# Raw output weights in four tiles instead of one, and their squares in four parts

## The chip, the cores and the metric

The kernel runs on one core of one Trainium2 chip. The metric is the device time of one execution in microseconds; three executions of the kernel before took 661.33, 661.75 and 663.46 us, so its time is the median, 661.75 us. The profile is of one execution more.

An engine's name in the profile stands for: PE, TensorE's matrix products, and PEld, its loading of weights; DVE, VectorE; ACT, ScalarE; POOL, GpSimd; SP, SyncE, which issues the DMAs.

## The reference

One decoder layer over 8 sequences of 128 tokens of width 512, in float32. Three blocks, each added to the residual `x`:

```python
x = x + attn(layernorm(x), w_q, w_k, w_v, w_o)        # 32 query heads, 8 key/value heads, of 128; causal
x = x + xattn(ctx, ctx, layernorm(x))                 # one head over the 128 context rows
x = x + ffn(layernorm(x), gate, up, down)             # 4-bit weights; silu(gate) * up, inner width 1376
```

What matters here is the first block's end. With `P[h]` the softmax of the masked and scaled scores of head `h`, the block adds

```python
attn = concat_h(P[h] @ V[h // 4])     # [8, 128, 4096]
x    = x + attn @ w_o                 # w_o: [4096, 512], 8 MB
```

so each group of 4 query heads that shares a key/value head multiplies its own 512 rows of `w_o`, 1 MB.

## The kernel before, in words

**Numbers.** Each product of two float32 matrices is made of three float16 products: both factors are split into a high and a low half (`split`, lines 116 and 119, and `convert`), and `mm3` (lines 162 to 164) adds high x high, high x low and low x high in PSUM. Before it is split a weight is multiplied by a scale that keeps it in float16's range. The scale of a block of weights comes from its sum of squares: `sumsq` squares the block on ScalarE and lets ScalarE sum along the row into one column of `ss` (line 260; what is written out, `junk`, is not used), and `scales_parts` casts the columns to bfloat16 (`sb`, line 283), adds them over rows and columns with one-column matmuls against a matrix of constants (`ps_n`, line 287 or 290), and makes the scale of it (lines 296 to 312, `sco` for the output weights). `convert` then multiplies the raw weights by the scale in place on GpSimd (line 356), casts them on ScalarE (`woh`) and subtracts on GpSimd (`wol`). Two of the 32 blocks are converted directly, on ScalarE and VectorE (lines 350 and 351), and read the raw weights without writing them.

**Units and steps.** The attention goes through 16 units, pairs of a group of heads (8) and a half of the batch (2 x 4 sequences); each unit has 4 steps, one a sequence: 64 steps. A unit is followed by the other half of its group; of the last two groups first both first halves run, and then both second halves. In step `i` the kernel makes the scores of step `i+1` (`att_s`), a piece of the projections for the unit after (`proj_piece`), the output product of step `i-1` (`att_o`, `ps_o`) and the product of probabilities and values of step `i` (`att_v`, `ps_at`, cast and split into `ah` and `al`). The scores are masked and scaled on VectorE (line 607), exponentiated on ScalarE (564), multiplied by the reciprocal sums on GpSimd (574 and 621), split (`pb`) and transposed by a DMA from SyncE (`pt`, line 635).

**Weights.** What a step has to prepare of coming weights is written in a table, filled by `at(step, ...)` in a loop over the groups (lines 1115 to 1142) and read at the end of each step. For the output weights of group `g`, whose first unit has number `u0`, with `c = 4 * (u0 - 1)` and `m = c - 4`: the load is issued at step `m`, the squares are made at `m + 1` and `m + 2`, the scale at `m + 3`, and the four blocks of 128 rows are converted at `c` to `c + 3` (`prep_wo`). A step below zero counts as 0. For groups 2 to 6, `m` is the step after the one in which the previous group's last block is converted. For group 7, `m` is the step in which group 6's first block is converted. Group 0 is loaded, squared and scaled in the opening (`begin`), which writes its instructions' order out by hand on every engine.

**Places.** A tile with `bufs=1` has one place in SBUF; whoever writes it next must wait until everything that reads it is done. `rawo` is one such tile of 128 x 4 x 512 float32. The load of group `g` so waits until the last of the four blocks of group `g - 1` has been converted, by `wol` on GpSimd as a rule.

**Order.** The program states no order beyond what data and places ask, but for the opening, and for a few edges: `issue_after` puts a square behind the exponentials, and a multiply of the raw weights behind the multiply of the probabilities, of the step that has just been written (`pace`). A planner that simulates the engines with its own estimates of durations then lays down a fixed order for each engine and for SyncE's issues; at run time every engine and SyncE take their instructions in that order and wait where something is not ready. From step 53 on GpSimd's order, and TensorE's until step 59, follow the text.

**DMAs.** Nearly all go out from SyncE: the weight loads, `pt`, duplicates of values (`vd`), and, in steps 8 to 41, the pieces of the quantized feed-forward weights and their zeros (`qr` and `zi`, lines 790 and 798).

Of the kernel before, what the change touches and what calls it, by code (L numbers as in the profile page):

```python
# [8 lines left out]
F32 = mybir.dt.float32  # L9
# [8 lines left out]
P = 128  # L18
HQ = 64
B = 8  # L20
H = 512
KT = 4
NG = 8
GH = 4
NH = 32
HB = 4
TH = 512
# [26 lines left out]
def tile_decoder(  # L54
# [19 lines left out]
    nc = tc.nc  # L74

    def pool(name, bufs=1, **kw):
        return tc.alloc_tile_pool(name=name, bufs=bufs, **kw)
# [12 lines left out]
    for k in range(2):  # L90
        m = const.tile([P, (k + 1) * HQ], F32, name=f"mask{k}")
# [95 lines left out]
    def bank(tag, shape, name):  # L187
        return psum.tile(shape, F32, name=name, tag=tag, bufs=BANKS[tag])
# [7 lines left out]
    rawp = pool("raw", 2)  # L196
# [13 lines left out]
    raw_t = {}  # L210
    sc_t = {}
# [22 lines left out]
        )  # L234

    def fetch_wo(g):
        raw_t["o", g] = raw = rawp.tile([P, GH, H], F32, name="rawo", tag="rawo", bufs=1)
        nc.sync.dma_start(
            raw, wo[g * TH : (g + 1) * TH, :].rearrange("(j p) c -> p j c", p=P)
        )  # L240

    def sumsq(kind, g, i, j, n=1):

        raw = raw_t[kind, g]
        if kind == "q":
            view = raw[:, :, j * P : (j + 1) * P]
        elif kind == "c":
            view = raw.unsqueeze(1)
        elif kind in "kv":
            view = raw  # L250
        else:
            view = raw[:, i * GH // n : (i + 1) * GH // n, :]
        key = "ss", kind, g
        if key not in raw_t:
            cols = GH if kind == "q" else n
            raw_t[key] = small.tile([P, cols], F32, name="ss" + kind, tag="ss" + kind)
        col = j if kind == "q" else i
        junk = work.tile([P, 2 * TH], BF16, name="junk", tag="junk", bufs=1)
        free = view.shape[1] * view.shape[2]
        ins = nc.scalar.activation(  # L260
            junk[:, :free].rearrange("p (a t) -> p a t", a=view.shape[1]),
            view,
            AF.Square,
            accum_out=raw_t[key][:, col : col + 1],
        )
        if pace:
            issue_after(ins, pace["exp"])
        return ins
# [79 lines left out]
    def convert(hi, lo, raw, sc, direct=False):  # L348
        if direct:
            a = nc.scalar.activation(hi, raw, AF.Copy, scale=sc)  # L350
            b = nc.vector.scalar_tensor_tensor(lo, raw, sc, hi, ALU.mult, ALU.subtract)
            return a, b
        wide = sc
        while len(wide.shape) < len(raw.shape):
            wide = wide.unsqueeze(2)
        a = nc.gpsimd.tensor_tensor(  # L356
            raw, raw, wide.to_broadcast(list(raw.shape)), ALU.mult
        )
        if pace:
            issue_after(a, pace["mul"])  # L360
        b, c = split(hi, lo, raw, nc.gpsimd)
        return a, b, c
# [21 lines left out]
    def prep_wo(g, j, direct=False):  # L384
        hi = wop.tile([P, H], F16, name="woh", tag="woh")
        lo = wop.tile([P, H], F16, name="wol", tag="wol")
        wo_t[g * GH + j] = hi, lo
        return convert(hi, lo, raw_t["o", g][:, j, :], sc_t["o", g], direct)

    def transpose4(src, tag):  # L390
        ps = bank(tag, [P, KT, P], "ps_x")
# [423 lines left out]
    for m in "gud":  # L815
        _, _, _, ngr, n = quant[m]
# [9 lines left out]
    def begin():  # L826

        warm = const.tile([P, TH], BF16, name="warm")
        nc.vector.memset(warm, 0.0)
        psw = bank("s", [P, TH], "ps_w")  # L830

        def fill(n):
            for _ in range(n):
                nc.tensor.matmul(psw, warm[:, :P], warm, start=True, stop=True)

        fill(11)
        load_x(0)
        load_x(1)
        fetch_wk(0)
        for b in range(2, HB):  # L840
            load_x(b)
        fetch_wq(0)
        fetch_wv(0)
        for b in range(HB, B):
            load_x(b)
        fetch_wo(0)
        fetch_wk(1)

        kgen = k_wide(0)
        h = {b: h_wide(b) for b in range(HB)}  # L850
        two = slice(0, TH // 2), slice(TH // 2, TH)
        q = [proj_q(0, 0, j, two if j == 0 else (slice(0, TH),)) for j in range(GH)]
        v = [proj_v(0, b) for b in range(HB)]
        ln_stats(0)
        ln_apply(0)
        ln_stats(1)
        ln_apply(1)
        sumsq("k", 0, 0, 0)
        next(h[0])
        fill(4)  # L860
        sk = scales_parts("k", 0)
        ln_stats(2)
        ln_apply(2)
        next(h[0])
        next(h[0])
        next(sk)
        next(h[1])
        fill(2)
        ln_stats(3)
        ln_apply(3)  # L870
        next(kgen)
        next(h[1])
        next(h[0])
        next(h[1])
        next(h[1])
        next(sk)
        next(h[2])
        next(kgen)
        sumsq("q", 0, 0, 0)
        next(h[2])  # L880
        next(h[2])
        sq0 = scales_parts("q", 0, (0, 1))
        next(sq0)
        sumsq("q", 0, 0, 1)
        next(h[3])
        next(kgen)
        next(sq0)
        next(h[3])
        next(h[2])
        sq1 = scales_parts("q", 0, (1, 2))  # L890
        next(sq1)
        next(h[3])
        prep_wq(0, 0, True)
        sumsq("q", 0, 0, 2)
        next(sq1)
        next(h[3])
        next(kgen)
        next(q[0])
        prep_wq(0, 1, True)
        sumsq("q", 0, 0, 3)  # L900
        sq = scales_parts("q", 0, (2, GH))
        ln_stats(4)
        ln_apply(4)
        next(q[0])
        next(sq)
        next(sq)
        next(kgen)
        prep_wq(0, 2, True)
        next(q[0])
        sumsq("v", 0, 0, 0)  # L910
        prep_wq(0, 3, True)
        h_dma(4)
        sv = scales_parts("v", 0)
        next(q[1])
        next(sv)
        ln_stats(5)
        ln_apply(5)
        next(q[1])
        next(sv)
        ln_stats(6)  # L920
        ln_apply(6)
        prep_wv(0, 0, True)
        h_dma(5)
        next(q[2])
        prep_wv(0, 1, True)
        next(q[2])
        ln_stats(7)
        ln_apply(7)
        h_dma(6)
        soft_scale(0)  # L930
        next(q[3])
        next(q[3])
        last_h = h_dma(7)
        fetch_wq(1)
        next(v[0])
        n = len(nc.cur_bb.bb.instructions)
        att_s(0, 0)
        loose.update(
            i.name for i in nc.cur_bb.bb.instructions[n:] if i.engine != mybir.EngineType.PE
        )  # L940
        next(v[1])
        next(v[0])
        prep_wk(0, True)
        next(v[2])
        next(v[1])
        next(v[3])
        next(v[2])
        next(v[3])
        run(proj_k(0, 1))
        run(proj_q(0, 1, 0))  # L950
        so = scales_parts("o", 0)
        for i in range(2):
            sumsq("o", 0, i, 0, 2)
        run(so)
        out_scale(0)
        prep_wo(0, 0, True)
        prep_wo(0, 1, True)
        return last_h

# [152 lines left out]
    def at(step, *fs):  # L1112
        todo.setdefault(max(step, 0), []).extend(fs)

    for g in range(1, NG):
        u0 = units.index((g, 0))
        c = HB * (u0 - 2)
        if g > 1:
            m = c - HB
            at(m, lambda g=g: fetch_wk(g))  # L1120
            at(m + 1, lambda g=g: (fetch_wq(g), sumsq("k", g, 0, 0)))
            at(m + 2, lambda g=g: (sumsq("q", g, 0, 0), sumsq("q", g, 0, 1)))
            at(m + 3, lambda g=g: (sumsq("q", g, 0, 2), sumsq("q", g, 0, 3)))
            at(m + 3, lambda g=g: (scales("q", g), scales("k", g), soft_scale(g)))
        for j in range(GH):
            at(c + j, lambda g=g, j=j: prep_wq(g, j))
        at(c + 1, lambda g=g: prep_wk(g))
        c = HB * (u0 - 1)
        m = c - HB
        at(m, lambda g=g: fetch_wo(g))  # L1130
        at(m + 1, lambda g=g: sumsq("o", g, 0, 0, 2))
        at(m + 2, lambda g=g: sumsq("o", g, 1, 0, 2))
        at(m + 3, lambda g=g: (scales("o", g), out_scale(g)))
        for j in range(GH):
            at(c + j, lambda g=g, j=j: prep_wo(g, j))
        if g % 2 == 0:
            c = HB * (u0 - 3)
            at(c - 2, lambda g=g: fetch_wv(g // 2))
            at(c - 1, lambda g=g: sumsq("v", g // 2, 0, 0))
            at(c, lambda g=g: scales("v", g // 2))  # L1140
            at(c + 2, lambda g=g: prep_wv(g // 2, 0))
            at(c + 3, lambda g=g: prep_wv(g // 2, 1))
# [332 lines left out]
```

## Time and profile before

| | us |
|---|---|
| median of three executions (from, to) | 661.75 (661.33, 663.46) |
| profiled execution, whole | 663.5 |
| its span, first to last instruction | 661.7 |
| TensorE busy | 631.9 |
| VectorE busy | 471.0 |
| ScalarE busy | 441.3 |
| GpSimd busy | 391.4 |
| 8 loads of `rawo`, 1 MB each, issue to landing where it is recorded | 5.6 |
| 16 squares of 128 x 1024 of `rawo`, median of one | 1.049 |
| 32 squares of 128 x 512 of `rawq`, median of one | 0.628 |

A line of a timeline or a group names the line of the kernel, the engine, the operation, what is written and read (`woh,ah` are the operands of `ps_o`), the shape, and how many; brackets at the end hold the idle time of the engine before it and who ended it. A matrix product's end is modelled and overlaps the next one's start, so holes in TensorE's work are best read from start to start. In the answer for one tile, the first list is time in which the engine of such an instruction sat idle before it, by what ended the wait, and the second is time in which others sat idle for it.

### The profile page before, as it was taken

The numbers are of one execution on the slowest core, as the hardware profiler recorded it, in microseconds if no ns is written. First come the engines' busy times: TensorE is split into PE (matmuls) and PEld (weight loads), VectorE is DVE, ScalarE is ACT, GpSimd is POOL, SyncE is SP. The second block draws the span as 40 slices with busy tenths as digits, with TensorE's granted clock in tenths as the row PEclk, the third lists the DMA queues.
The fourth block names the chain that finished last, engine by engine and source line by source line (L and its number), as shares of the span: only waits on it lengthen the run. The fifth ranks groups of instructions, "written<-read, shape, count | busy, mean of one in ns | idle before, by whom it ended". The sixth has DMA issues, their size and how long they took to land.

```text
span 661.7 us, 12423 instructions
## 1 busy us (share of the span) xinstructions
PE 631.9 (95%) x3992; PEld 340.9 (52%) x3992; DVE 471.0 (71%) x1476; ACT 441.3 (67%) x1240; POOL 391.4 (59%) x581
## 2 busy tenths in 40 slices
PE   8889999899999999999999999999998988999996
PEld 5545545455655555555555565455554444445443
DVE  6846786556767776675767565777676668978897
ACT  5676677565758574666678566865566478876674
POOL 6658497664747795556588597753577247621521
PEclk9999999999999999999999999999999999999999
DMA  8266244945453855445546514243534243102002
GB/s 309 49 162 163 87 46 131 235 99 158 120 158 83 187 133 153 108 148 140 156 115 146 148 37 124 47 103 69 88 61 70 41 87 53 32 17 63 2 1 63
DMA packets 117773, 69.34 MB, mean 105 GB/s; under 512 B 84190, under 2 KB 100593, under 8 KB 117708
## 3 DMA queue, kind: packets, MB, share of 16 engines
q1 hardware_dynamic: 117708, 68.55, 42.7%
q8 instruction: 31, 0.51, 0.3%
q14 instruction: 34, 0.28, 0.1%
HBM read 42.12 MB, written 2.20 MB: 67 GB/s over the span
## 4 chain that ended last, share of the span: by engine, by line
PE 49%; POOL 15%; DMA 10%; DVE 9%; issue 8%; ACT 7%; SPq 0%; DVEq 0%; POOLq 0%; ACTq 0%
PE ps_c L1176 6%; PE ps_c L1177 6%; PE ps_o L164 5%; PE ps_o L162 5%; PE ps_o L163 5%; PE ps_q L164 4%; PE ps_q L163 4%; PE ps_q L162 4%; DMA pt<-pb 3%; POOL pb L119 3%; DMA rawq<-in_L_attn_w_q_dram 3%; POOL s L621 3%; DMA rawo<-in_L_attn_w_o_dram 2%; POOL wql L119 2%; ACT junk L260 2%
## 5 line engine op out<-in xcount | busy, mean ns | idle before, releaser
L564 ACT ACTIVATE s<-s,negm 128x64 f32<-128x64 f32 (+1 forms) x256 | 93.0, 365 | 32.8 <-DVE negm L607 32.5
L162 PE MATMUL ps_o<-woh,ah 128*128 128x512 f16 x256 | 97.1, 379 | 2.3 <-ACT ah L116 2.2
L162 PE MATMUL ps_q<-hT,wqh 128*128 128x512 f16 (+1 forms) x260 | 97.7, 376 | 1.4 <-ACT wqh L350 1.4
L164 PE MATMUL ps_o<-woh,al 128*128 128x512 f16 x256 | 97.0, 379 | 1.2 <-DVE al L119 1.2
L164 PE MATMUL ps_q<-hT,wql 128*128 128x512 f16 (+1 forms) x260 | 97.7, 376 | 0.0
L163 PE MATMUL ps_q<-hT,wqh 128*128 128x512 f16 (+1 forms) x260 | 97.7, 376 | 0.0
L163 PE MATMUL ps_o<-wol,ah 128*128 128x512 f16 x256 | 97.0, 379 | 0.0
L119 POOL TENSOR_TENSOR pb<-s,pb 128x256 f16<-128x256 f32 (+1 forms) x128 | 71.7, 576 | 13.0 <-ACT pb L116 10.6
L661 DVE SCALAR_TENSOR_TENSOR xr<-ps_o,unsc,xr 128x512 f32<-128x512 f32 x64 | 47.8, 747 | 41.7 <-PE ps_o L164 41.1
L574 POOL TENSOR_SCALAR rec<-rec 128x4 f32<-128x4 f32 x64 | 14.8, 231 | 95.5 <-DVE rec L572 93.7
L607 DVE CUSTOM_DVE_ANT_0 s<-ps_sc,mask,soft 128x64 f32<-128x64 f32 (+1 forms) x256 | 66.8, 310 | 5.3 <-PE ps_sc L164 2.5
L621 POOL TENSOR_TENSOR s<-s,rec 128x128 f32<-128x128 f32 (+1 forms) x128 | 63.8, 519 | 4.5
L119 DVE TENSOR_TENSOR ql<-ps_q,qh 128x512 f16<-128x512 f32 x64 | 43.9, 686 | 31.2 <-ACT qh L116 31.0
L116 ACT CAST pb<-s 128x256 f16<-128x256 f32 (+1 forms) x128 | 43.0, 350 | 31.7 <-POOL s L621 29.1
L116 ACT CAST ah<-ps_at 128x512 f16<-128x512 f32 x64 | 37.1, 581 | 23.2 <-PE ps_at L164 9.5
L119 DVE TENSOR_TENSOR al<-ps_at,ah 128x512 f16<-128x512 f32 x64 | 43.7, 683 | 6.7 <-ACT ah L116 6.2
L564 ACT ACTIVATION_READ_ACCUMULATOR s<-s,negm 128x1 f32 x256 | 48.2, 188 | 0.0
L116 ACT CAST qh<-ps_q 128x512 f16<-128x512 f32 x64 | 36.7, 573 | 13.9 <-PE ps_q L164 13.9
L1189 DVE TENSOR_SCALAR ps_c<-ps_c,rTg 128x512 f32<-128x512 f32 (+1 forms) x56 | 40.6, 750 | 7.0 <-PE ps_c L1177 6.0
L1187 ACT ACTIVATE ps_c<-ps_c,rTu 128x512 f32<-128x512 f32 (+1 forms) x57 | 36.3, 659 | 13.7 <-PE ps_c L1177 11.8
L356 POOL TENSOR_TENSOR rawo<-rawo,sco 128x512 f32<-128x512 f32 x30 | 31.4, 1053 | 22.2 <-DVE sco L312 20.1
L164 PE MATMUL ps_sc<-k,ql 128*128 128x64 f16 (+1 forms) x256 | 42.8, 206 | 1.0 <-DVE ql L119 1.0
(239 smaller groups left out, 1725.9 us busy)
## 6 DMA issues: line engine op xcount, KB each, us to landing
rawq<-in_L_attn_w_q_dram SPq DMA_DIRECT2D x8, 1024.0 KB
rawo<-in_L_attn_w_o_dram SPq DMA_DIRECT2D x8, 1024.0 KB, 5.6
zi<-zd SPq DMA_DIRECT2D x26, 256.0 KB, 4.1
vd<-v SPq DMA_DIRECT2D x64, 64.0 KB, 2.9
qr<-_L_ffn_down_qweight_dram SPq DMA_DIRECT2D x10, 256.0 KB
xr<-in_x_dram SPq DMA_DIRECT2D x8, 256.0 KB, 8.6
rawk<-in_L_attn_w_k_dram SPq DMA_DIRECT2D x8, 256.0 KB, 4.4
rawv<-in_L_attn_w_v_dram SPq DMA_DIRECT2D x4, 512.0 KB
```

The costliest lines, as they stand in the source:

```text
L116: a = nc.scalar.copy(hi, src)
L119: b = (lo_eng or nc.vector).tensor_tensor(lo, src, hi, ALU.subtract)
L162: nc.tensor.matmul(ps, lh, rh, start=start and i == 0, stop=False)
L163: nc.tensor.matmul(ps, lh, rl, start=False, stop=False)
L164: nc.tensor.matmul(ps, ll, rh, start=False, stop=stop and i == n - 1)
L564: exp = nc.scalar.activation(v, v, AF.Exp, bias=negm[:, j : j + 1], scale=-1.0, accum_out=sums[:, j : j + 1],)
L607: nc.vector.tensor_tensor_reduce(view, flat(ps, cols[j]), masks[j // 2], soft_t[g][:, j % 2 : j % 2 + 1], BIG, ALU.add, ALU.min, negm,)
L621: mul = nc.gpsimd.tensor_tensor(v, v, rec[:, 2 * k : 2 * k + 2].unsqueeze(2).to_broadcast([P, 2, (k + 1) * HQ]), ALU.mult,)
L661: return nc.vector.scalar_tensor_tensor(xr[b], ps, unsc_t[g], xr[b], ALU.mult, ALU.add)
L1176: nc.tensor.matmul(ps, lh, rh, start=r == 0, stop=False, skip_group_check=r > 0)
L1177: nc.tensor.matmul(ps, lh, rl, start=False, stop=True, skip_group_check=r > 0)
L1189: nc.vector.tensor_scalar(ps, ps, sc, None, ALU.mult)
```

## The change

`rawo` becomes four tiles of 128 x 512 float32, with tags `rawo0` to `rawo3`, each with one place of its own; together they take the room of the one before. A new function, `fetch_wo_part`, loads one of them, 256 KB. In the table, part `j` of a group is loaded at step `m - 3 + j`; so the parts of groups 2 to 6 are asked for one by one in the step after that in which the previous group's block `j` is converted (`fetch_wo`, which loads all four, remains for group 0). For group 7 the steps are 41 to 44, and group 6's blocks are converted in steps 44 to 47, so there each part has to wait for its place. For group 1 the four steps are all step 0.

The sum of squares is made of four parts of 512 elements, at steps `m`, `m + 1`, `m + 1` and `m + 2`, with four columns in `ss` and so four one-column matmuls in `scales_parts` (whose code is not touched). The scale stays at `m + 3` and the conversions at `c` to `c + 3`. In the opening group 0 is loaded by four DMAs and squared in four parts.

```diff
     def fetch_wo(g):
-        raw_t["o", g] = raw = rawp.tile([P, GH, H], F32, name="rawo", tag="rawo", bufs=1)
-        nc.sync.dma_start(
-            raw, wo[g * TH : (g + 1) * TH, :].rearrange("(j p) c -> p j c", p=P)
-        )
+        for j in range(GH):
+            fetch_wo_part(g, j)
+
+    def fetch_wo_part(g, j):
+        raw = rawp.tile([P, H], F32, name="rawo", tag=f"rawo{j}", bufs=1)
+        raw_t.setdefault(("o", g), []).append(raw)
+        nc.sync.dma_start(raw, wo[g * TH + j * P : g * TH + (j + 1) * P, :])
...
-            view = raw[:, i * GH // n : (i + 1) * GH // n, :]
+            view = raw[i].unsqueeze(1)
...
-        return convert(hi, lo, raw_t["o", g][:, j, :], sc_t["o", g], direct)
+        return convert(hi, lo, raw_t["o", g][j], sc_t["o", g], direct)
...
-        for i in range(2):
-            sumsq("o", 0, i, 0, 2)
+        for j in range(GH):
+            sumsq("o", 0, j, 0, GH)
...
-        at(m, lambda g=g: fetch_wo(g))
-        at(m + 1, lambda g=g: sumsq("o", g, 0, 0, 2))
-        at(m + 2, lambda g=g: sumsq("o", g, 1, 0, 2))
+
+        for j in range(GH):
+            at(m - 3 + j, lambda g=g, j=j: fetch_wo_part(g, j))
+        for j in range(GH):
+            at(m + j - (j > 1), lambda g=g, j=j: sumsq("o", g, j, 0, GH))
         at(m + 3, lambda g=g: (scales("o", g), out_scale(g)))
         for j in range(GH):
             at(c + j, lambda g=g, j=j: prep_wo(g, j))
```

## The prediction

> **What bounds the kernel now.** I read first the page's busy times and its chain, then the waits of TensorE, then everything that touches the raw output weights (`rawo`), then the timelines of the engines where that showed a wait, and last the SyncE queue.
>
> From the page:
>
> ```profile
> PE 631.9 (95%) x3992; PEld 340.9 (52%) x3992; DVE 471.0 (71%) x1476; ACT 441.3 (67%) x1240; POOL 391.4 (59%) x581
> ...
> PE 49%; POOL 15%; DMA 10%; DVE 9%; issue 8%; ACT 7%; SPq 0%; DVEq 0%; POOLq 0%; ACTq 0%
> ```
>
> TensorE does work that the change leaves alone; the time can only fall by the holes between its matmuls. In a dense stretch 512-column matmuls start 0.22 us apart, so I count a hole from start to start. Between 40 and 500 us the holes over 0.4 us that could have to do with `rawo` are: 0.77 us at 66.50, 1.10 at 89.86, 1.84 at 124.25, 0.48 at 232.83, 1.71 at 415.36, 0.49 at 430.49. The other large ones lie after 440 us, in the last attention steps, cross attention and the feed-forward network.
>
> The answer for the tile `rawo`:
>
> ```profile
> its engine sat idle before it (us, times) until:
>   DVE sco L312: 20.1, 4
>   POOL rawo L356: 7.3, 13
>   DMA rawo<-in_L_attn_w_o_dram: 5.8, 2
> ...
>   ACT junk L260: 5.8, 2
> ```
>
> ScalarE twice stood still for the 1 MB load: 4.0 us before the square at 64.78 (load issued at 56.68, for group 1) and 1.8 us before the one at 411.64 (issued at 405.79, for group 7). The ScalarE timeline around the second:
>
> ```profile
> 409.44 0.41 ACT L116 CAST pb<-s 128x256 f16<-128x256 f32 x1 [0.27 <-POOL s L621]
> 411.64 1.06 ACT L260 ACTIVATE junk<-rawo 128x1024 bf16<-128x1024 f32 x1 [1.80 <-DMA rawo<-in_L_attn_w_o_dram]
> ...
> 414.75 0.56 ACT L116 CAST ah<-ps_at 128x512 f16<-128x512 f32 x1
> ```
>
> And TensorE:
>
> ```profile
> 413.44 0.38 PE L162 MATMUL ps_q<-hT,wqh 128*128 128x512 f16 x1
> 415.36 0.39 PE L162 MATMUL ps_o<-woh,ah 128*128 128x512 f16 x1 [1.55 <-ACT ah L116]
> ```
>
> The product `ps_at` that `ah` is cast from was complete at about 409.8, but the cast stood behind the square that waited for the load. That is 1.92 - 0.22 = 1.70 us of TensorE. At 64.78 the same happens: the cast `wkh`, ready when its multiply ended at 60.2, stands behind the square until 65.84, and TensorE has its 0.77 us hole at 66.50.
>
> For groups 2 to 6 there is no such wait: `sb` (the copy of the sums) is done at 115.06, 178.74, 238.24, 300.85 and 359.33, and its matmul `ps_n` comes at 133.83, 198.54, 254.34, 320.56 and 375.87. There 16 to 22 us are spare, so nothing that makes the sums earlier is worth anything. The "DVE sco 20.1" above is GpSimd waiting for a scale whose matmul stands late in TensorE's order, not for the load.
>
> **What the Trainium skill says.** "ScalarE: Activation LUTs", What ACT_TABLE_LOAD costs: an ACTIVATE with immediate scale and bias takes 186 ns + 0.833 ns an element, and neighbours overlap by some 93 ns. For 512 and 1024 elements that is 612 and 1039 ns; the trace's minima are 612 and 1039, it agrees. "Perfetto Trace Analysis", Tensor Engine Instruction: ScalarE, VectorE and GpSimd take their instructions strictly in order; the trace agrees: between 409.84 and 414.75 the exponentials and `ah` stand behind the square that waits. "DMA: Bandwidth & Descriptors", Anatomy of one DMA: about 2.0 us fixed plus bytes at 436 GB/s (fitted for loads issued by GpSimd), an estimate of 4.4 us for 1 MB and 2.6 for 256 KB. The trace has 5.65 us (97.70 to 103.35) for the first, and 3.4 to 4.4 us medians for 256 KB loads: longer in both. Same page, Queues, rings and completion order: each DMA engine takes a queue's descriptors in ring order. So a load issued ahead of a transpose delays it; the transpose at 404.49, with the 1 MB load just behind, landed after 4.6 us where others take 2.7 to 3.3.
>
> **The change part by part.**
> *Squares.* Two of 1024 elements become four of 512. In the timeline one of each occupies ScalarE from start to next start 1.05 and 0.63 us (with its accumulator read). 4 x 0.63 - 2 x 1.05 = +0.42 us a group, 3.4 us in all eight. ScalarE is 67% busy and does them a step at a time, so seven groups hide it behind ScalarE's idle third. Group 0 does not: from 43.8 to 54 us ScalarE is nearly full, and `ps_n` at 47.77 waited 0.76 us for `sb`, whose square ended at 47.5. There I charge the whole +0.42 us.
> *Sums.* `scales` now makes four one-column matmuls, not two. Their starts lie 27 ns apart (47.77, 47.79; 418.42, 418.45): 2 x 8 x 0.027 = +0.43 us on TensorE, hidden by nothing.
> *Loads.* 24 more issues at 0.43 to 0.57 us on SyncE, each of 256 KB. Parts 0 to 2 of groups 2 to 7 go out when their own last reader (`wol`, GpSimd) ends, 5 to 20 us earlier than the block did; part 3 where the block did. In the opening, SyncE is free from 8.9 to 22.8 us, so 3 x 0.48 there cost nothing; without that cover the second `rawk` load would be 1.4 us late, and it is used only at 53 us. Behind each new issue the next attention transposes `pt` and the dequantization loads wait 0.53 us. GpSimd releases `wol` and `pb` in its own order, and in the trace `wol` of parts 1 and 2 mostly ends after `pt` went out (215.49 against 213.50; 271.61 against 270.33; 337.68 against 335.95; 399.22 against 398.13), so the load follows the transpose. Part 0 comes before it (82.77 against 83.81; 206.09 against 207.31), where TensorE needs `pt` 5.7 us or more after its issue (in step 45 it needs it after 3.5, but there part 0 is 3.4 us ahead). Only at step 5 is that slack used up (6.05 us, hole 1.10 at 89.86, with the store of the zeros just ahead). The transfer of 256 KB takes 0.7 us at the 374 GB/s of the stretch 226 to 228; bounds 0 and +0.7, and I take +0.3 since transposes there move little (67 GB/s).
> *Stall of group 7.* When `wol` of part 3 ends at 405.6, parts 0 to 2 have been loaded since 389 to 403 and can be squared; only 256 KB are awaited, landing some 3.5 us later, 409.3, by when ScalarE first has room (409.84). Bounds: 0 if the planner again places the last square too early, -1.7 if not. I take -1.7. What is late next: the exponentials of the same step, which move up with it.
> *Stall of group 1.* Places 0 and 1 are free after `wol` on VectorE at 52.8 and not at 55.2, parts land before 62 even at the 8.0 us of this crowded stretch (0.7 of it data at full rate). `wkh` gets up to 3 us earlier: -0.77, bounds 0 and -0.77.
> *Traffic.* At 232.83 the hole waits for a `pt` that took 6 us because 1 MB of `rawo` (221.88) and 512 KB of `rawv` (223.22) were ahead; 768 KB of this go earlier, 2 us at 374 GB/s: -0.48.
> *Scale of group 7.* Its three multiplies bunch at 422.10 to 425.59 and push `pb`; the hole at 430.49 is behind that. The scale follows TensorE, which is earlier: -0.49, bounds 0 and -0.49.
>
> Sum: -1.71 - 0.77 - 0.48 - 0.49 + 0.42 + 0.43 + 0.30 = -2.3 us. The profiled execution took 663.5 us, its span 661.7 and 1.8 around it, so it becomes 661.2; the median of the runs, 661.75, lies with the span, and becomes 659.4. No other hole lies between to eat the 1.7 us: after 415 everything hangs on TensorE's own order.
>
> **The rivals.**
> *A, the sum:* 659.4, own range 657.5 to 660.3.
> *B, the wait stays:* the planner places the small squares as hopefully as the large ones (its two stalls of 4.0 and 1.8 us show that it thought the load faster than it was). A quarter of the load still needs its 3.5 us against 5.8. Then group 7 gives back 1.71 and 0.49: -0.1, so 661.6. For it: the stall itself. Against: three quarters can be squared first.
> *C, the transposes become late:* every part goes out ahead of its `pt`. Price: 0.53 us issue + 0.7 us transfer = 1.2 us in a step without slack. TensorE takes `pt` 3.89, 2.85, 3.45, 3.53 and 3.58 us after issue in steps 22, 30, 38, 45 and 46, where landing takes some 3: five such steps, +6.0 - 2.3 = +3.7, 665.4. It decides from the fourth step on (4 x 1.2 - 2.3 = +2.5). For it: the slack is really that small. Against: GpSimd's order, above.
> *D, the planner's order shifts elsewhere:* all of ScalarE's, VectorE's and SyncE's order is planned anew. One example is in the trace: `pt` of step 10 was ready at 117.99 and went out at 119.98 behind a dequantization load that waited for its place, hole 1.84. If it vanishes with A, 657.5; if two or three new ones of its kind come, -2.3 + 2.5 x 1.9 = +2.4, 664.2.
> That the loads do not come earlier at all can't be: each part has its own place, and SyncE already issues loads as soon as a place is free (97.70 after a `wol` ending 97.49).
>
> **How the numbers follow.** A 0.50, B 0.14, C 0.16, D downward 0.10, D upward 0.10. A measurement of this kernel tells some 0.3%, 2.0 us, from no change: of A 0.40 lies below 659.8 and 0.10 inside. Faster 0.40 + 0.10 = 0.50; same 0.10 + 0.14 = 0.24; slower 0.26. Range 655.5 to 666.0: below, D and A with their bounds; above, C with its 5 steps; the ends leave out D with four holes and C with more.
>
> **What would show it.** Right: no wait of ScalarE for `rawo` over 1 us near 65 and 410; `ah` cast within 1 us of the end of its `ps_at` there; TensorE without the holes at 66 and 415; the first three loads of each group well ahead of the fourth. Wrong: waits of TensorE for `pt` above the present 5.0 us (C), a square of part 3 still waiting near 409 (B), new SyncE waits ahead of `pt` (D), or `ps_n` of group 0 late by more than 0.5 us.

## The result, and the profile after

The change makes the kernel slower: 667.15 us (median of five, 665.74 to 668.78) against 662.76 for the kernel before, run in between on the same chip; ratio 1.0057, 95% interval 1.0029 to 1.0085. 659.4 was predicted, with 666.0 as the upper end. Repeated in a later comparison, it gave 1.0058 (1.0035 to 1.0082).

The page of the changed kernel, its busy times and its chain (whose shares add up to 37%, so that most of the span is in no part of it; it is not used here):

```profile
PE 634.7 (95%) x4008; PEld 342.3 (51%) x4008; DVE 475.9 (71%) x1476; ACT 442.9 (67%) x1272; POOL 392.2 (59%) x581
...
PE 18%; DVE 5%; ACT 5%; POOL 4%; DMA 3%; issue 2%; DVEq 0%; POOLq 0%; ACTq 0%
```

16 more matrix products and 32 more ScalarE instructions, as planned, in a span of 665.9 us instead of 661.7. The answer for the tile `rawo`, cut to the waits:

```profile
L263 ACT ACTIVATE junk<-rawo x32: 612/628/641, 45.3 to 412.1; 128x512 bf16<-128x512 f32 x32
...
  DVE sco L315: 24.7, 5
  POOL rawo L359: 5.7, 12
  DMA rawo<-in_L_attn_w_o_dram: 5.1, 6
...
DMA to landing us min/median/max: 2.5/2.8/5.4
```

ScalarE's two long waits for the load (5.8 us) have become six short ones (5.1 us). But the hole of TensorE at 415.36 is gone, and from 405 to 447 us no hole of TensorE is over 0.3 us. ScalarE's last square of group 7, the cast `ah` of the same step and TensorE's product behind it:

```profile
412.08 0.63 ACT L263 ACTIVATE junk<-rawo 128x512 bf16<-128x512 f32 x1 [0.90 <-DMA rawo<-in_L_attn_w_o_dram]
...
416.35 0.57 ACT L116 CAST ah<-ps_at 128x512 f16<-128x512 f32 x1
```

```profile
416.97 0.39 PE L162 MATMUL ps_o<-woh,ah 128*128 128x512 f16 x1
```

Ahead of that stretch a hole of 0.65 us is new, which the profile puts down to `ql`:

```profile
397.11 0.27 PE L162 MATMUL ps_v<-wvh,hT 128*128 128x256 f16 x1 [0.48 <-DVE ql L119]
```

The cast `qh` that `ql` is made from stood at 395.75 near the end of a run of ScalarE's work without a pause, which began at 391.57 with a wait of 0.61 us for the first part of group 7. The hole is there in all eight profiles that load group 7 in four early parts (0.59 to 0.65 us), and in none of the others; no run tests its cause.

The answer for `c`, the context rows of the cross attention, which ScalarE squares in the same stretch; first of the kernel before, whose two lines say 1.1 us in one wait:

```profile
its engine sat idle before it (us, times) until:
...
  DMA c<-in_ctx_dram: 1.1, 1
```

and after:

```profile
its engine sat idle before it (us, times) until:
  DMA c<-in_ctx_dram: 6.2, 3
```

On ScalarE's timeline of the changed kernel, with the idle time in brackets, the three waits and what stands behind them:

```profile
431.56 0.63 ACT L263 ACTIVATE junk<-c 128x512 bf16<-128x512 f32 x1 [2.05 <-DMA c<-in_ctx_dram]
...
436.68 0.63 ACT L263 ACTIVATE junk<-c 128x512 bf16<-128x512 f32 x1 [2.28 <-DMA c<-in_ctx_dram]
437.21 0.19 ACT L263 ACTIVATION_READ_ACCUMULATOR junk<-c 128x1 f32 x1
437.30 0.57 ACT L116 CAST ah<-ps_at 128x512 f16<-128x512 f32 x1
...
444.88 0.63 ACT L263 ACTIVATE junk<-c 128x512 bf16<-128x512 f32 x1 [1.85 <-DMA c<-in_ctx_dram]
445.42 0.19 ACT L263 ACTIVATION_READ_ACCUMULATOR junk<-c 128x1 f32 x1
445.51 0.57 ACT L116 CAST ah<-ps_at 128x512 f16<-128x512 f32 x1
```

It is the picture of 411.64 in the kernel before, with another load: a square that waits, and the cast `ah` that TensorE needs behind it. TensorE's timeline at the last of them:

```profile
446.49 0.38 PE L163 MATMUL ps_o<-wol,ah 128*128 128x512 f16 x1
447.85 0.39 PE L164 MATMUL ps_o<-woh,al 128*128 128x512 f16 x1 [0.99 <-DVE r L307]
```

1.15 us lost. `r` is named because it came last on VectorE; `al`, which the product reads, was made at 447.11 to 447.80 from the `ah` of 445.51.

**Where the time went, place by place.** I took the first product `ps_at` of each step as a landmark and subtracted the landmarks of before. The columns are the changed kernel, its second profile (e1), the changed kernel with five places for `c` (e7, below), and what the steps of the prediction put there:

| stretch | after | e1 | e7 | predicted |
|---|---|---|---|---|
| start to step 0 | +0.74 | +1.59 | +0.46 | +0.42 |
| step 0 to 2 | +0.54 | +0.54 | +0.54 | 0 |
| 2 to 9 (holes at 66.50 and 89.86) | +0.12 | +0.15 | +0.13 | -0.47 |
| 9 to 23 | +0.13 | +0.19 | -0.06 | 0 |
| 23 to 24 (hole at 232.83) | -0.49 | -0.49 | -0.49 | -0.48 |
| 24 to 29 | +0.04 | +0.04 | +0.04 | 0 |
| 29 to 30 (hole at 273.19) | +1.73 | +0.81 | +0.73 | 0 |
| 30 to 43 | +0.04 | +0.05 | +0.05 | 0 |
| 43 to 54 (holes at 415.36 and 430.49) | +1.25 | +1.01 | -1.75 | -2.20 |
| 54 to the end | +0.10 | +0.33 | +0.37 | 0 |
| all | +4.20 | +4.22 | +0.02 | -2.73, and +0.43 of sums in all stretches |

The first row is not a steady one. The inputs arrive at other times in each execution (the third normalized block starts between 8.03 and 9.28 us), and in the two profiles of the first two columns TensorE ran at half its clock for 3.4 us near 20 us. Such windows are in every kernel's runs: over the timed runs the mean granted clock was 0.9956 for the kernel before (56 runs) and 0.9963 for the changed one (11), so they do not make the difference. Two rows were not foreseen, 29 to 30 and 43 to 54.

How far one profile can be trusted is seen in e5 and e9 (below), which load and square the output weights as the kernel before does; but for ten small products e5 has its order to the end, and e9 has it up to step 43. Against before they show +0.08 and -0.64 us in steps 2 to 9 and -0.48 and -0.49 in steps 23 to 24, and e5 shows -0.64 in steps 43 to 54. So half a microsecond in one of these rows, the -0.49 of the changed kernel included, is no more than two executions of one order can differ by.

### The profile page after: what moved, and what is told of

It is laid out like the page before. It is cut to its first block, busy times and chain, and to the rows that moved or that the text cites. A ratio compares the mean times of both kernels' runs of the same rounds, so it can differ in the third digit from the quotient of the medians.

```text
span 665.9 us, 12550 instructions
## 1 busy us (share of the span) xinstructions
PE 634.7 (95%) x4008; PEld 342.3 (51%) x4008; DVE 475.9 (71%) x1476; ACT 442.9 (67%) x1272; POOL 392.2 (59%) x581
## 5 line engine op out<-in xcount | busy, mean ns | idle before, releaser
L164 PE MATMUL ps_sc<-k,ql 128*128 128x128 f16 (+1 forms) x256 | 42.9, 206 | 1.1 <-DVE ql L119 1.0
```

Source lines behind the costliest of these rows:

```text
L164: nc.tensor.matmul(ps, ll, rh, start=False, stop=stop and i == n - 1)
```

## The experiments

The theories. **T1**: the early loads change what SyncE issues before the transposes, at steps 5 and 30. **T2**: four squares cost ScalarE time where it has none. **T3**: the small squares of group 7 stall ScalarE as the large ones did; later sharpened to **T3b**: the stall was replaced by the waits for `c`. **T4**: the half clock in the opening is what differs. **T5**, formed after the first four runs: a packet of TensorE's own instructions falls on the transpose of step 30. Each kernel was compared with the kernel before on the same chip; the ratios and intervals are those comparisons.

**e1, the changed kernel again.**

> The changed kernel, unaltered. Every theory: about 667 us, some 4.4 above the kernel before. What it tells apart: in the first profile of the changed kernel TensorE had a granted clock of 0.5 for 3.4 us in the opening (19.4 to 22.8 us), which no execution of the kernel before showed. If that is chance (theory T4), this profile lacks it, its span is about 1 us shorter, and the holes of steps 5 (about 2.0 us) and 30 (about 2.4 us) are there all the same. If it belongs to the change, it is there again.

667.72 against 663.69; 1.0058 (1.0035 to 1.0082). The half clock was there again (19.41 to 22.82 us), but it is no mark of the change: 8 of the 16 profiles told of here show it near 18 to 20 us, two of them with the loads and squares of before (e5, e9), and before's own runs average the lower clock. T4 falls. The holes were 1.99 at step 5 and 1.50 at step 30.

**e2, the kernel before with the squares in four parts.**

```diff
-        at(m + 1, lambda g=g: sumsq("o", g, 0, 0, 2))
-        at(m + 2, lambda g=g: sumsq("o", g, 1, 0, 2))
+        for j in range(GH):
+            at(m + 1 + j // 2, lambda g=g, j=j: sumsq("o", g, j, 0, GH))
```

(and four in the opening.)

> The kernel before with the squares in four parts and nothing else: one tile, one load of 1 MB as before. T1 (the early loads change SyncE's order, and that is the loss: holes at steps 5 and 30, +2.6 us) expects little, 662.8 to 663.8, the hole of step 5 at 1.1 us and that of step 30 at 0.7. T2 (four squares cost ScalarE time where it has none: the opening, +0.7, and the four one-column matmuls, +0.4) expects 663.9 to 665, with the delay of step 0 at +0.7 as in the changed kernel. T3 (group 7's small squares stall ScalarE as the large ones did and spoil steps 44 to 53, +1.3) expects the hole of 1.7 us before the output product of step 47 to stay or shift.

665.50; 1.0030 (1.0013 to 1.0046), half of the loss, with the loads as before. T1 cannot be the main cause. Nor is it T2's opening: step 0 came at -0.35. The profile loses 1.6 us at one place, the hole of step 30, which went from 0.69 to 2.27 us although SyncE's order around it is the same to the instruction. Steps 43 to 54 are 0.56 us longer, and before two squares of `c` ScalarE waited 1.23 and 1.71 us.

**e3, two tiles of 512 KB, two squares.**

```diff
-        at(m, lambda g=g: fetch_wo(g))
+        for i in range(2):
+            at(m - 2 + 2 * i, lambda g=g, i=i: fetch_wo_half(g, i))
```

> Two tiles of two blocks, each half of 512 KB loaded when its place is free (two and no steps ahead of the old place); two squares of 1024 columns as before. T1 expects SyncE's order to move again, with a load going out ahead of the transposes of steps 5 or 30: holes there of 1.5 us or more, 664 to 666. T2 expects the opening as before and no loss: 661 to 662.8. T3 expects group 7's wait before a square to shrink from 1.8 us to under 1: 661.

663.17; 0.9984 (0.9965 to 1.0003). Early loads without extra squares lose nothing: against T1. The hole of step 30 was 0.63. In group 7 the waits grew instead, 2.93 and 2.51 us before the two squares, and the hole at 415.66 was 2.17: T3's expectation for this run was wrong.

**e4, the changed kernel with the four loads together at the old place.**

```diff
-        for j in range(GH):
-            at(m - 3 + j, lambda g=g, j=j: fetch_wo_part(g, j))
+        at(m, lambda g=g: fetch_wo_late(g))
```

(`fetch_wo_late` issues parts 3, 0, 1 and 2 one after the other; squares at `m + 1` and `m + 2`.)

> The changed kernel with its four tiles and four squares, but the four loads go out together at the old place of the block, the fourth part first. T1 expects the holes of steps 5 and 30 to fall back to 1.1 and 0.7 us, and the time to about 664.5; T2 expects no gain, 667, since the squares are the same; T3 expects the loss of steps 44 to 53 to stay or to grow, since the parts land later, 664.5 to 666.

665.75; 1.0035 (1.0020 to 1.0051). Step 5 as T1 said: hole 0.91 instead of 1.96. Step 30 not: 1.68. Steps 43 to 54 lost 1.31 us, and before three squares of `c` ScalarE waited 1.69, 2.76 and 1.82 us.

**What is at step 30.** The hole is there when the transpose lands late. In the page, DMA queues are named by number and kind; `q8 instruction` carries 31 packets of 16 KB in every kernel, one each 15 to 31 us. TensorE has 3,992 products and as many loads of weights, 258 for a packet; no other engine has a quarter of that, so I read q8 as TensorE's program being fetched. The view of the DMAs between the issue of the transpose and its landing, for the kernel before (271 to 274 us):

```profile
q1 hardware_dynamic: 984, 0.43, 56.6%
issues: line engine op xcount, KB each, median us to landing
```

and after (272 to 276 us; the first two lines are the busy share in tenths and the rate, in 40 slices):

```profile
DMA  0000027999999900000000010000029999890998
GB/s 0 0 0 0 0 46 166 212 207 200 205 182 225 10 0 0 0 0 0 0 0 0 8 10 8 8 10 10 10 41 266 305 452 492 348 348 20 389 492 280
...
q8 instruction: 1, 0.02, 1.5%
```

The transpose moves at 200 GB/s until 273.3, when a fetch begins on one DMA engine and takes 0.96 us; for 1.6 us almost nothing moves, and the last pieces of the transpose come after that. That they are those of the engine with the fetch is my reading; the trace does not name the engines. In the kernel before the fetch came at 275.6, when nobody needed it. The 16 added sums are two instructions each, loading weights and multiplying: by step 30 TensorE's program is 20 instructions longer, and the fetch comes earlier. To test it, nothing but TensorE's program has to get longer.

**e5, the kernel before with ten one-column products at the start.**

```diff
         fill(11)
+        for _ in range(10):
+            nc.tensor.matmul(psw[:, :1], warm[:, :P], warm[:, :1], start=True, stop=True)
```

> The kernel before with ten added one-column matmuls among the warm-up matmuls at the start (their result is never read); the order of every engine is otherwise the same. They take about 0.3 us where TensorE waits for its first input anyway, and move everything behind them by 20 instructions in TensorE's stream, as far as the sixteen added sums have moved it by step 30. T5 (one 16 KB packet of TensorE's instructions, every 17 to 22 us, lands on top of the transpose of step 30 and holds it up) expects that packet near 271 us instead of 275.6, the transpose of step 30 landing 1 to 1.8 us later, the hole there 1.6 to 2.4 us instead of 0.7, and about +1 to +1.7 us in all, 664.5 to 665.5. T1 (SyncE's order) and T2 (ScalarE's squares) expect nothing, 663.7, with the hole at 0.7.

TensorE's line of step 30 in the kernel before, and then in e5:

```profile
273.19 0.27 PE L644 MATMUL ps_at<-pt,vd 128*128 128x256 f16 x1 [0.52 <-DMA pt<-pb]
```

```profile
274.32 0.27 PE L644 MATMUL ps_at<-pt,vd 128*128 128x256 f16 x1 [1.92 <-DMA pt<-pb]
```

The order of every other engine is that of before, and the packet came at 271.38 instead of 275.62: it is TensorE's. The lost time went from 0.69 to 2.09, steps 29 to 30 +1.40. T5 holds at its place. The whole time did not follow: 663.98; 0.9999 (0.9982 to 1.0015).

**e6, the changed kernel with sixteen of them.**

> The changed kernel with sixteen such one-column matmuls at the start, all else in the same order: 32 more instructions, so that the packet that lay on the transpose of step 30 comes some 3.5 us earlier. T5 expects the hole of step 30 to fall from 2.4 (1.5 in the second profile) to 0.7 us, perhaps also a shorter hole at step 10, and 666 to 666.7 against 667.7. T1 expects the hole of step 30 to stay at 1.5 or more and the time at 667.7, since SyncE's order is that of the changed kernel.

```profile
277.96 0.27 PE L647 MATMUL ps_at<-pt,vd 128*128 128x256 f16 x1 [0.43 <-DMA pt<-pb]
```

The fetch came 0.2 us before the transpose was issued, and 0.60 us is lost instead of 2.41 (1.50 in e1). 667.19; 1.0044 (1.0028 to 1.0061), against 1.0058 without the sixteen: lower by 0.9 us, less than the two intervals can tell.

**e7, the changed kernel with five places for `c`.**

```diff
-        raw_t["c", b] = c = xc.tile([P, H], F32, name="c", tag="c", bufs=3)
+        raw_t["c", b] = c = xc.tile([P, H], F32, name="c", tag="c", bufs=5)
```

> The changed kernel with five places instead of three for the context rows c of the cross attention, whose loads then go out earlier. T3b (the stall of ScalarE for the weights of group 7 was only replaced by its waits for c: 2.05, 2.28 and 1.85 us before three of its squares, with the casts of steps 49 to 52 behind them) expects these waits to vanish, the holes of 1.15 and 0.62 us at 447.9 and 453.6 to shrink, and 666 to 666.9 against 667.7. If the time stays at 667.7 with the waits gone, these holes have another cause. T1 and T2 expect no change.

663.99; 1.0004 (0.9988 to 1.0021): 0.54% less than the 1.0058 of e1, 3.6 us, give or take 1.9. Its answer for `c`:

```profile
its engine sat idle before it (us, times) until:
  ACT cp L353: 1.9, 4
  DMA c<-in_ctx_dram: 0.8, 1
```

The holes at 447.85 and 453.60 are gone. The casts `ah` of steps 50 and 51, which came 2.87 and 3.42 us after their `ps_at` was complete in the changed kernel (1.74 and 2.98 before), come 0.04 us after it, and steps 43 to 54 give -1.75 us where the changed kernel lost 1.25. More than expected, since these two holes alone were 1.8 us; the whole stretch went into another order with it.

**e9, the control: five places in the kernel before.**

> The control for the run with five places for c: the kernel before with five places for c and nothing else. T3b (the changed kernel lost 3.7 us to waits for c that the kernel before hardly has: 1.1 us before one square) expects 663 to 663.9 against 663.8, so that the five places are worth much to the changed kernel alone. If the kernel before gains 3 us as well, the waits for c are no part of what the change did, and the change loses 4 us elsewhere.

663.52; 1.0006 (0.9991 to 1.0022). No difference that the measurement tells. So the places are worth 3.6 us to the changed kernel alone; as to what the waits for `c` cost, T3b holds.

**e8, the two tiles of e3 with five one-column products.**

> The kernel with two tiles of 512 KB (663.2) with five one-column matmuls at the start, all else in the same order: 10 more instructions, about 1 us. T5 expects the packet of instructions that lay on the transpose of step 10 (at 121.3 us, the transpose issued at 120.65) to come before it, the hole of step 10 to fall from 1.84 to about 0.9 us, the hole of step 30 to stay at 0.6, and 662.2 against 663.2. Without T5 nothing moves.

The expectation failed, in T5's favour. 665.95; 1.0029 (1.0014 to 1.0044), which is 3.0 us more than e3, give or take 1.6, for five products of 27 ns and no other change of order (each was compared with the kernel before on its own chip; the two profiled executions, 664.11 and 664.40 us, do not show the difference). At step 10 the hole fell from 1.84 to 1.35. At step 30 the fetch, which I had thought would move by 1 us, moved by 3 with respect to the transpose and landed on it. TensorE's timeline:

```profile
270.09 0.22 PE L164 MATMUL ps_sc<-k,ql 128*128 128x128 f16 x1
272.57 0.37 PE L650 MATMUL ps_at<-pt,vd 128*128 128x256 f16 x1 [2.26 <-DMA pt<-pb]
272.74 0.63 PE L162 MATMUL ps_q<-hT,wqh 128*128 128x512 f16 x1
273.16 0.63 PE L163 MATMUL ps_q<-hT,wqh 128*128 128x512 f16 x1
273.59 0.63 PE L164 MATMUL ps_q<-hT,wql 128*128 128x512 f16 x1
```

2.42 us lost before `ps_at`, and behind it the products start 0.43 us apart, not 0.22: the granted clock was 0.5 from 272.52 to 275.93. From step 29 to 31 this execution lost 3.4 us against before.

**e10, the first load of each group behind the transpose of its step.**

```diff
+        if j == 0 and i > 0:
+            issue_after(ins, pt_dma[steps[i]])
```

> The changed kernel with the first of the four loads of each group held behind the transpose of its step in SyncE's order, all else as it was. T1, reduced to step 5 (the load of part 0 goes out ahead of the transpose, and the hole is 2.0 us there instead of 1.1), expects the hole of step 5 at 1.1 us and about -0.9 us, 666.8 against 667.7; the holes of steps 44 to 54 stay. If the hole of step 5 stays at 2.0, the store of the zeros alone makes it.

666.19; 1.0045 (1.0030 to 1.0060). (`i` is the step in whose table the load stands.) The hole of step 5 fell only from 1.96 to 1.78. SyncE's order at step 5 in the changed kernel shows why the first expectation was too simple:

```profile
83.18 0.34 SPq L243 DMA_DIRECT2D rawo<-in_L_attn_w_o_dram  x1
83.74 0.26 SPq L785 DMA_DIRECT2D zd<-z  x1
84.20 2.13 SPq L638 DMA_TRANSPOSE pt<-pb  x1
86.42 0.81 SPq L243 DMA_DIRECT2D rawo<-in_L_attn_w_o_dram  x1
```

Between the load and the transpose stands `zd`, the store of the zeros: 19 packets of 5,504 bytes, which all show up one after the other over some 5 us. In every profile TensorE starts on the transpose 1.2 to 1.4 us after the store's last packet (1.85 in e2), so I take it that the transpose's share on that way comes last. Before, the store ran from 83.70 to 88.64; after, with 256 KB ahead of it, from 85.40 to 90.37; with the load behind both, from 84.82 to 90.50. The load costs here on either side. Only where none is near (e4) is the hole short. T1 is right about this step: the hole is 1.77 to 1.99 us in the six profiles with an early load there (after, e1, e6, e7, e10, e11) and 1.07 to 1.53 in the four with the loads of before (before, e2, e5, e9). That is 0.9 us at most.

**e11, the three remedies together** (e7, e10 and sixteen products).

> All remedies together on the changed kernel: five places for c, the first load of each group behind the transpose of its step, and sixteen one-column matmuls at the start that take the packet of instructions off the transpose of step 30. From the kernel with five places (664.0): -0.9 at step 5 and -0.7 at step 30, 662.4. If the three causes are the right ones, it is faster than the kernel before (663.8) by 1 to 2 us; what is left of the loss is then the 0.4 us of sums and the later holes.

664.34; 1.0012 (0.9996 to 1.0028): 2 us above the expectation, no better than e7. The hole of step 30 was 0.59, steps 43 to 54 -1.74; step 5 was still 1.77, and a hole of 0.45 came up at 311.

**e12, the two tiles with five places.**

> Two tiles of 512 KB (663.2) with five places for c. T3b expects its waits for c (0.8 and 3.0 us before two squares) to vanish, but not the 2.2 us hole at 415.7, which belongs to the waits of 2.9 and 2.5 us before the large squares of group 7: 662 to 663.

662.61; 0.9994 (0.9984 to 1.0005). The waits before squares of `c` were 0.3 and 1.2 us, the hole at 414.6 still 2.08. Neither it nor e3 can be told from the kernel before.

**e13 and e14: early loads for group 7 alone, five places; without and with sixteen products.**

```diff
+        if g < NG - 1:
+            at(m, lambda g=g: fetch_wo_late(g))
...
+        else:
+            for j in range(GH):
+                at(m - 3 + j, lambda g=g, j=j: fetch_wo_part(g, j))
...
```

(The squares of groups 1 to 6 are made as in e4.)

> Four tiles and four squares, five places for c, but only group 7 loads its parts early; groups 1 to 6 load theirs together at the old place, the fourth part first. If the causes are the right ones: the hole of step 5 at 0.9 us, steps 44 to 54 gained 1.7 us (as with the early loads and five places), a hole of 1.4 to 2.4 us at step 30 if the packet of TensorE's instructions falls within 1 to 2 us of the transpose, and 0.7 if not. From the late loads (+2.3 against the kernel before), -3 us in steps 44 to 54: -0.7 us, 662.5 against 663.2.

> The same with sixteen one-column matmuls at the start, all else in the same order. T5 expects the packet of instructions to come before the transpose of step 30 is issued, its hole to fall to 0.6 or 0.7 us, and 1.0 to 1.5 us less than without them in time too: 661.3, faster than both kernels. If the hole falls in the profile and the time stays, the hole's price is not what it looks like there.

664.66 and 663.57; 1.0011 (0.9997 to 1.0024) and 0.9994 (0.9979 to 1.0010). In e13 step 5 was at 0.94 as expected, step 30 at 2.01 with the fetch 1.2 us after the transpose, but steps 43 to 54 gave only -0.87: ScalarE's waits for the loads of group 7 now made holes of 1.07 and 0.59 at 391 and 396. In e14 the fetch came first, the hole of step 30 was 0.58, and the medians differ by 1.1 us in the expected direction. No version tried is faster than the kernel before by more than the measurement tells.

**All traces of step 30 together.** In nine profiles (after, e1, e2, e4, e5, e7, e8, e10, e13) the fetch began 0.98 to 2.11 us after the transpose was issued, and TensorE could start 3.64 to 4.63 us after the issue. In seven (before, e3, e6, e9, e11, e12, e14) it began before the issue or more than 5.1 us after it, and TensorE started after 2.78 to 2.85. There is no exception. What it costs in the whole time is less clear. With the fetch on the transpose instead of off it: e8 against e3 3.0 us more (the two intervals together 1.6 wide to each side), e13 against e14 1.1, e1 against e6 0.9, e5 against before -0.1 (1.1 to each side). By these medians it costs something between nothing and the 1.8 us by which the hole grows, and perhaps more where a half clock follows.

## Why the prediction was wrong

*The stall of group 7* is the step that failed, and in it two sentences: that what is late next are the exponentials of the same step, and that after 415 everything hangs on TensorE's own order. The hole of 1.71 did vanish, and that of 0.49, as forecast. But ScalarE then stood before the squares of `c`, whose loads wait for one of three places; the last went out at 442.15, just after the multiply that freed it. These waits are 6.2 us, with casts that TensorE needs behind them. Forecast for the stretch were -2.20 us, measured +1.25 and +1.01; with the places there (e7, e11) -1.75 and -1.74. I looked for other holes of TensorE in the way, and not for the other waits of the engine that was to be freed, though the trace of before had one of 1.1 us for `c` in that stretch.

What these waits cost is shown by e7 with e9 as its control. That they came because ScalarE had been freed is not: in e4 ScalarE still waits for group 7 (1.94 and 0.57 us) and TensorE still has a hole of 1.57 us there, and yet the waits for `c` are 6.5 us; in e2, with the loads of before and a hole of 1.72, they are 2.9 us. Early loads, small squares and the order that the planner lays anew all came together, and the runs do not separate them.

*Transposes (+0.30, bounds 0 and 0.7).* The hole of step 5 grew by 0.86: just outside. What was mis-sized is the term: the load delays the store that stands ahead of the transpose, and shares its way with it. Rival C took place in this one step, and not in the five that it needed.

*Step 30 (nothing forecast).* +1.73 and +0.81, and T5's fetch is shown to make it by e5, e6, e8 and e14. I did count the 16 sums as work (16 x 27 ns), and not as 32 instructions that move all later ones in the program. Rival C's 665.4 came nearest to the measured time, by luck. Rival D's upward case, 664.2, named the kind of cause, an order planned anew with a load that waits for its place, but not the tile: its example was another.

*Rival B* was half right: the planner did place small squares before their loads had landed (0.61, 0.21, 1.15 and 0.90 us in group 7, 2.9 us in all against 1.8 before). The cast `ah` of step 47, which was to follow its product within 1 us, came 2.77 us after it (4.90 before); TensorE had other products in the meantime. So the hole went, though the sign that was named for it did not appear.

*Right by its number, not shown in its mechanism:* the traffic at 232.83, forecast -0.48, measured -0.49 in all three columns. TensorE's line in the kernel before, in e5 and in e9:

```profile
232.83 0.28 PE L644 MATMUL ps_at<-pt,vd 128*128 128x256 f16 x1 [0.32 <-DMA pt<-pb]
```

```profile
232.57 0.27 PE L644 MATMUL ps_at<-pt,vd 128*128 128x256 f16 x1
```

```profile
233.79 0.27 PE L644 MATMUL ps_at<-pt,vd 128*128 128x256 f16 x1
```

In e5 and e9 the same 1 MB goes out ahead of the transpose as before, and the hole is missing. It is 0.00 to 0.49 us in the seven profiles with late loads (before, e2, e4, e5, e9, e13, e14) and 0.00 in the nine with early ones. The direction may be right; the size was that of one execution.

The hole at 66.50 is gone too, and TensorE is busy without a break from 60 to 80 us. But e2 and e9, with the load of before, do not have it either (e9 still waits 2.99 us for the load), while e5 has 0.89 us. It is no fixed price.

*Right:* the sums. Steps without another change, such as 20 to 21 and 27 to 28, are in the kernels with four squares longer by 0.05 to 0.06 us, two sums of 27 ns. The squares of the opening were put at +0.42; steps 0 to 2 show +0.52 to +0.61 in every kernel with four squares and 0.00 in every one with two, though at a hole (56.94, before `ps_v`) that I had not named, so the size is right and the place is not.

The sum said -2.3 and the span grew by 4.2. Of these 6.5 us, 3.45 lie in steps 43 to 54, 1.73 at step 30, 0.6 in steps 2 to 9, 0.9 before step 2, which is partly chance; and any of these may be off by half a microsecond.

*Readings that were off, without consequence:* the time to spare in groups 2 to 6 is 16.1 to 19.8 us, not 16 to 22. The loads of 256 KB have medians of 3.4 to 8.6 us on the page of before, not 3.4 to 4.4; the parts of `rawo` took 2.8. The transpose at 404.49 has its load behind it, and is no example of a load ahead. Step 14, where TensorE takes the transpose 2.91 us after its issue, belongs on rival C's list.

## What to carry to other kernels

When a wait is taken from an in-order engine, list every other wait on that engine in the next stretch, even short and harmless ones, and ask which loads cannot come earlier. Here two more places for such a load were worth 3.6 us, but only in the changed kernel. Instructions that cost almost nothing still move the rest of the program: look at when the packets of instructions come before blaming a stall on the edit that stands next to it. And repeat the profile, of the kernel before as well: in the opening arrival times alone differ by a microsecond, and two of the holes that the change seemed to remove are missing in runs with the old loads.

## What the runs showed of the hardware

TensorE's instructions are fetched during the run, in packets of 16 KB that each hold one DMA engine for 0.9 to 2.1 us. Where one began 1 to 2.1 us after the transpose of step 30 was issued, TensorE could start on the transpose 3.64 to 4.63 us after the issue, and otherwise after 2.78 to 2.85. Ten products of 27 ns at the start of the program brought a fetch 4 us earlier (e5), without a change in the whole time that the measurement tells; five brought one 3 us earlier with respect to the transpose (e8), in a kernel that took 3.0 us more, give or take 1.6.

A hole of TensorE can be followed by 3.413 us at half clock. The Trainium skill, "TensorE: Matmul & The Clock Gate", What's actually happening, describes free-running windows of 3413 ns, which agrees with every such stretch here but the one at the end of each run (3.413, in one case 6.827); in HAM oscillation — how this bites in real kernels, it warns of gaps above some 3.4 us. Here a half clock followed shorter ones: gaps of 2.01 to 2.26 us in five of nine cases, and the one of 1.39 us near 19 us in eight of sixteen, while some 70 other gaps of 1.1 to 1.98 us had none. So a hole near 2 us may cost its own length, or that and up to 1.7 us more (an estimate: half of 3.413 us); what decides is not shown.
